# Another order of the steps in a two-layer graph kernel, with one buffer moved between two pools

## The chip, the core and the metric

The kernel runs on one core of one Trainium2 chip. The core has a matrix engine (TensorE, "PE" in the profile, with the loads of its stationary operand shown apart as "PEld"), three engines for elementwise work (VectorE "DVE", ScalarE "ACT", GpSimd "POOL") and a sync engine whose queue issues nearly all transfers ("SP"). PE writes its sums to eight banks of PSUM; DVE and ACT take them out to SBUF, where everything else lies. The metric is the device time of one execution in microseconds (us), taken as the median of several runs.

## The reference

The input is 128 graphs of 128 nodes with 512 features (`x`) and a 128 x 128 weighted adjacency matrix for each (`adj`). All numbers are 32-bit floats. Two layers follow each other, each with a residual sum and a layer norm:

```python
# layer 0
deg = sum(adj, -1);  agg = (adj @ x) / max(deg, 1e-6)
x = layernorm(x + relu(concat([x, agg]) @ W.T))            # W is 512 x 1024
# layer 1: three graph convolutions
h = relu(adj @ (x @ W1) + b1)
h = relu(adj @ (h @ W2) + b2)
x = layernorm(x + adj @ (h @ W3) + b3)                      # W1, W2, W3 are 512 x 512
```

So each graph meets five 512 x 512 weight matrices (the two halves of `W`, then `W1`, `W2`, `W3`) and its adjacency matrix four times.

## The kernel before

**Tiling.** Four graphs form a group, and there are NG = 32 groups. The large products are not done directly. They are done with the fast scheme that multiplies 2 x 2 blocks with seven products in place of eight, and for most of the weight matrices a second time inside each of the seven. The sums of blocks that the scheme needs are made ahead: by `sums` (outer level) and `inner_sums` (inner level, whose results go to small buffers called `ti`, three forms each). The inner forms of the two halves of `W` don't fit into SBUF and are streamed from device memory for every group, into a ring of six buffers (tiles `ring` and a part of `big`).

**Steps.** The work of one group is cut into 22 stages, whose names are used below:

- X, D, AT: load the transposed `x` and its sums; load the adjacency matrix and make the degrees; load the transposed adjacency matrix.
- L0 to L3: `x` times both halves of `W` (lines 875 to 878). L0 and L1 do the first four of the seven outer places, L2 and L3 the rest. A stage has seven products; a product of L is 4 matmul records of 256 columns (2 for L3).
- A0, A1: for two graphs each, adjacency times the result, relu, residual, layer norm (`seg_agg`, lines 880 to 903).
- G0 to G3: adjacency times the normalized result, one graph each (`seg_g1`).
- Ha, Hb: times `W1`, one level of the scheme only, so products of 8 records of 256 columns (line 596).
- Sa, Sb: times `W2`; H2: adjacency (`seg_h2`); Ta, Tb: times `W3`. A product is 8 records of 128 columns in Sa and Ta and 6 in Sb and Tb (line 614).
- Z0, Z1: adjacency, bias, residual, layer norm, and the way out (`seg_last`).

A stage is a generator, and each `yield` ends one step, mostly one product with what takes its result out of PSUM. In `first_part` (lines 630 to 665), which Sa, Ta, L0 and L1 use, the seven products come in the order 1, 5, 6, 2, 7, 4, 3. Products 1, 6, 7 and 4 add up in one bank, `py`, and ACT copies that bank out in between, so product 7 waits for the copy of what product 6 left (`copied`, line 576). `last_part` does the same for the other three places, and starts 5 from a bank that ACT fills first (line 698).

**Order.** Three things make the order of the instructions.

1. `ORDER` lists the steps of one period, 104 of them: `L3-4` means one step of stage L3 for the group that is four behind the period's number. A step whose stage is not yet allowed by `AFTER` goes to a list `late` and is taken as soon as it is allowed (lines 1218 to 1239). `AFTER` says what must be finished: Sa of a group needs Z0 and Z1 of the group before, Ha needs Tb of the group before, L0 needs A0 and A1 of the group before, and so on.
2. The list so made is a plan's input. `deadlines` (lines 78 to 93) gives each PE step a due time, the sum of the PE times ahead of it in the list, and every other operation the due time that its users leave it. An operation with no user is given `REST` us.
3. `order` (lines 95 to 223) plays the engines against each other with estimated durations. PE takes the first of its next `AHEAD` steps that is ready and has its buffers (lines 176 to 183). The other engines take the earliest due. DVE takes over a sum meant for POOL when it is due within `HELP` us (lines 191 to 196). A transfer or filling with a lead may not start more than that lead ahead of its due time: `LEADS` holds that for fillings of banks, loads of `x`, first inner sums and ring loads. The instructions are then put out in this order, and each engine runs its own in order.

**Buffers.** `SIZES` counts the `s` buffers (512 columns: banks copied out, loads of `x`, results on the way out), the `v` buffers (partial sums of a first part), the `ti` buffers (inner forms of the data) and the ring. A pair of places takes one `ti` buffer, so one operand of L, S or T takes four of them. The planner lets a load of `x` take an `s` buffer only when more than three are free.

Of the kernel before, what the change touches and what calls it, by code (L numbers as in the profile page):

```python
# [35 lines left out]
class Plan:  # L36
# [5 lines left out]


    LAG = 0.15
    AHEAD, HELP, HOLD, SEEN, REST, SPARE = 32, 16.0, 5.0, 8, 15.0, 1
    DMA_US, DMA_RATE = 2.0, 0.22e6

    def __init__(self, pools):
# [175 lines left out]


BANKS = 8
SIZES = 8, 3, 7, 6
LEADS = 6.9, 7.0, 29.0, 448.5
AFTER = {
    "X": "L2-1+1 L3-1+1", "D": "A0-1 A1-1 D-1", "AT": "Z0-2 Z1-2", "L0": "X D AT A1-1 A0-1 Z0-2 Z1-2", "L1": "L0", "L2": "L1", "L3": "L1 L2<2",  # L230
    "A0": "L2 L3", "A1": "L2 L3", "G0": "A0 Hb-1", "G1": "A0 Hb-1", "G2": "A1 Hb-1", "G3": "G0 G1 G2 A1",
    "Ha": "G3 Tb-1!", "Hb": "Ha", "Sa": "Hb Z0-1! Z1-1!", "Sb": "Sa", "H2": "Sb", "Ta": "H2", "Tb": "Ta", "Z0": "Ta Tb!", "Z1": "Tb",
}
ORDER = """
    L3-4 L0-4 Ta-6 H2-5 L3-4 Tb-5 Sa-5 L1-4 L1-4 Hb-5 D Tb-6 L2-4 L3-4 G0-4 Z0-6 Sb-4 D L2-4 L2-4 Tb-5 L0-3 L0-3 L1-4
    Ta-5 Ha-4 A1-4 L1-4 L3-3 Tb-5 Sb-4 X-3 Tb-5 A0-4 Ha-4 L2-4 L3-3 Ha-4 Ha-4 H2-5 H2-5 H2-5 Hb-4 L0-3 Tb-5 Tb-5 H2-5
    L3-4 L2-4 L2-4 Sb-4 L1-3 L2-4 L0-3 Z1-6 Sb-4 L3-3 Ta-5 Sb-4 Ta-5 G3-4 AT-3 A0-3 Ta-5 G2-4 Z0-5 L3-3 Z0-5 G2-4 Sa-4
    Ha-3 Ta-5 Tb-5 A1-4 Ha-3 Sb-4 G1-4 Sa-4 Sb-4 L0-3 G3-4 Sb-4 L1-3 Sa-4 Sa-4 Sa-4 Sa-4 Z1-5 A0-4 L1-3 G1-4 Z1-6 L2-3
    Hb-4 G0-4 AT-3 Ta-5 X-2 L1-3 Ta-5 L0-3 A1-3 Sa-4 L0-3
"""  # L240


# [1 line left out]
def gnn_resnorm_kernel(  # L244
# [24 lines left out]

    NS, NV, NI, NR = SIZES  # L270
    EARLY = 2
# [35 lines left out]
    def pinned(ins):  # L307
        return tc.keep_in_program_order(ins)
# [4 lines left out]
    def scalar(n, emit, reads, writes, columns=0, lead=None):  # L313
        plan.op("ACT", 0.165 + 0.00083 * n + 0.1 * columns, emit, reads, writes, lead=lead)

    def dma(dst, src, reads, writes, size, queue="SP", lead=None):
        eng = nc.sync if queue == "SP" else nc.scalar
        plan.op(queue, 0.06, lambda: pinned(eng.dma_start(dst(), src())), reads, writes, size=size, lead=lead)  # L318

    def const(v):  # L320
        return lambda: v

    def add(eng, n, dst, a, b, reads, writes, op=OP.add, shared=False, lead=None):

        on_vector = lambda: pinned(nc.vector.tensor_tensor(dst(), a(), b(), op=op))  # L325
        if eng == "POOL":
            on_gpsimd = lambda: pinned(nc.gpsimd.tensor_tensor(dst(), a(), b(), op=op))  # L327
            plan.op("POOL", 0.03 + 0.00243 * n, on_gpsimd, reads, writes, True, other=(0.06 + 0.00123 * n, on_vector), lead=lead)
        else:
            vector(n, on_vector, reads, writes, shared)  # L330
# [90 lines left out]
    class Streamed:  # L421

        def parts(self, ps, i):
# [3 lines left out]
                lambda: RING_T[s.index][:, 0:n], const(FORMS[i - 1][:, ps[0] : ps[-1] + 1].rearrange("p k s n -> p k (s n)")),  # L427
                ["ring free"] + [("form", w, i, p) for w in range(2) for p in ps], [s], n * P * H * 4, lead=LEADS[3],
            )
            return [lambda j=j: RING_T[s.index][:, j] for j in range(n)], [s]  # L430

    class Data:
# [18 lines left out]
        def inner_sums(self):  # L451
            for ps in PAIRS:
# [13 lines left out]
                for dst, a, b, reads, writes, op in (  # L466
# [4 lines left out]
                ):  # L471
                    add("POOL", n * P, dst, a, b, reads, writes, op, lead=LEADS[2] if dst is first else None)

# [91 lines left out]
    def bank_ap(s):  # L565
        return BANK[s.index]

    def quarters(p, n):
        return bank_ap(p).rearrange("p a (b n) -> p (a b) n", n=P)[:, 0:n]
# [50 lines left out]
    def v_part(v, n, g, c):  # L620
        return lambda: V_T[v.index][:, 0:n, g, c]
# [56 lines left out]
    def last_part(a, b, ps, joint, v, kv, sinks):  # L678
# [18 lines left out]

        scalar(n * P, lambda: pinned(nc.scalar.copy(quarters(pz, n), v_part(v, n, 1, 1)())), kv, [pz], lead=LEADS[0])
        add("POOL", n * P, v_part(v, n, 0, 1), v_part(v, n, 0, 1), v_part(v, n, 1, 1), kv, [(v, "d")], OP.subtract)
# [180 lines left out]
    def seg_agg(q, m):  # L880
        y, u = l0(q)
        for g in (2 * m, 2 * m + 1):
            p, r = Slot("bank", seeded=True), Slot("s", spare=3)
            dma(lambda r=r: S_T[r.index].rearrange("p a b -> p (a b)"), const(x[q][:, g]), (), [r], P * F * 4, lead=LEADS[1])
            scalar(512, lambda g=g, p=p: pinned(nc.scalar.copy(bank_ap(p), u.graph(g))), u.keys((g,)), [p], lead=LEADS[0])
            plan.op(
# [211 lines left out]
    def seg_last(q, m):  # L1098
# [3 lines left out]
        for j, o in enumerate(os):  # L1102
            g = 2 * m + j
            p = Slot("bank", seeded=True)
            scalar(512, lambda p=p: pinned(nc.scalar.copy(bank_ap(p).rearrange("p a b -> p (a b)"), B3_T)), ["b3"], [p], lead=LEADS[0])
            plan.op(
# [181 lines left out]
```

## Time and profile before

| | |
|---|---|
| median of 3 runs | 2265.83 us (2265.13 to 2266.15) |
| the profiled execution | 2261.35 us, its span 2259.4 us |
| PE busy | 2238.6 us (99%), 13620 matmul records |
| weight loads | 1967.4 us (87%) |
| DVE, ACT, POOL busy | 72%, 55%, 49% |
| DMA | 147 GB/s on average; the main queue's packets 47.5% of the 16 engines |

The span is what the profile's page covers; the execution's own time has 1.95 us more around it. The median of the runs is 4.5 us above the profiled execution. In the middle of the kernel the picture repeats every 69.59 us: the group of 44 records that begins at 1038 us of the chain is at 1107 and 1177 us again. This is the period, one group of graphs. A record's time as the page gives it includes the way through the array, so records overlap: a row of 8 records of 128 columns is listed with 1.06 us, and the next row begins 0.89 us after it began. Where the next row begins later than that, PE has lost time. This is how the rows below are to be read.

### The profile page before, as it was taken

Reading aid. Unit: us, or ns where it says so; the run is one execution under the profiler, and the core shown is the slowest. Engines: PE = TensorE matmul, PEld = TensorE weight load, DVE = VectorE, ACT = ScalarE, POOL = GpSimd, SP = SyncE. Lnnn points to the kernel's source line nnn. Section 1 sums busy time; section 2 is a strip of 40 time slices with the busy share of each in tenths; the row PEclk is TensorE's granted clock in tenths of the full one; section 3 lists DMA queues with packets and bytes.
Section 4 is the critical chain, followed back from the end, with each engine's and each line's share of the span. In section 5 each row is a group of like instructions: output and inputs, shape, how many; then the busy total and the mean of one; then the engine's idle time right before and its main releaser. Section 6 shows DMA issues by size and latency. Waiting matters only on the chain.

```text
span 2259.4 us, 39677 instructions
## 1 busy us (share of the span) xinstructions
PE 2238.6 (99%) x13620; PEld 1967.4 (87%) x13620; DVE 1632.7 (72%) x3552; ACT 1237.8 (55%) x2369; POOL 1112.0 (49%) x1400
## 2 busy tenths in 40 slices
PE   8999999999999999999999999999999999999998
PEld 7888888898898988988888889889898898888886
DVE  5677777777777777777777777777777777777675
ACT  2455555555555555555555555555555555555554
POOL 0245554545545455454555454654545545455540
PEclk9999999999999999999999999999999999999999
DMA  7744445534455444554444553445534455443431
GB/s 236 158 139 133 138 155 172 168 122 146 130 180 175 122 147 134 167 171 137 139 135 158 171 164 123 144 137 176 179 117 151 130 167 171 131 135 127 157 120 38
DMA packets 218615, 333.12 MB, mean 147 GB/s; under 512 B 39344, under 2 KB 84400, under 8 KB 218416
## 3 DMA queue, kind: packets, MB, share of 16 engines
q1 hardware_dynamic: 217744, 330.33, 47.5%
q8 instruction: 110, 1.80, 0.4%
q14 instruction: 89, 0.73, 0.2%
q10 hardware_dynamic: 672, 0.26, 0.1%
HBM read 290.46 MB, written 40.04 MB: 146 GB/s over the span
## 4 chain that ended last, share of the span: by engine, by line
PE 98%; DMA 1%; DVE 0%; issue 0%; ACT 0%; SPq 0%; ACTq 0%; DVEq 0%
PE bank L614 58%; PE bank L596 21%; PE bank L914 5%; PE bank L1002 5%; PE bank L1109 5%; PE bank L889 5%; DMA s<-in_x_dram 1%; DMA big<-in_w0T_dram 0%; DVE st L828 0%; DVE u L896 0%; DVE big L325 0%; SPq L318 0%; ACTq L1283 0%; ACT u L859 0%; ACT T L1013 0%
## 5 line engine op out<-in xcount | busy, mean ns | idle before, releaser
L576 ACT COPY s<-bank 128x384 f32<-128x384 f32 (+1 forms) x567 | 306.2, 540 | 428.7 <-PE bank L614 327.3
L596 PE MATMUL bank<-T,w 128*128 128x256 f32 x1792 | 411.7, 379 | 0.0
L596 PEld LDWEIGHTS bank<-T,w 128*128 128x128 f32 x1792 | 335.8, 190 | 68.9 <-issue 28.5
L327 POOL TENSOR_TENSOR xT<-xT 128x512 f32<-128x512 f32 (+1 forms) x244 | 236.6, 970 | 137.6 <-DVE ah L325 41.4
L325 DVE TENSOR_TENSOR v<-bank,s 128x512 f32<-128x512 f32 x240 | 162.7, 688 | 191.5 <-PE bank L614 133.9
L327 POOL TENSOR_TENSOR T<-T 128x512 f32<-128x512 f32 (+2 forms) x250 | 253.0, 1028 | 69.5 <-ACT T L925 38.1
L614 PE MATMUL bank<-big,ti 128*128 128x128 f32 (+1 forms) x1410 | 261.7, 317 | 0.0
L614 PE MATMUL bank<-big,xT 128*128 128x256 f32 x976 | 253.9, 380 | 1.1 <-DMA big<-forms 1.1
L582 ACT COPY bank<-bank 128x512 f32<-128x512 f32 (+2 forms) x273 | 142.9, 523 | 176.7 <-PE bank L614 124.4
L614 PEld LDWEIGHTS bank<-w,ti 128*128 128x128 f32 x1680 | 215.9, 192 | 18.9 <-issue 7.2
L614 PEld LDWEIGHTS bank<-big,T 128*128 128x128 f32 x1680 | 215.9, 191 | 15.5 <-issue 7.0
L327 POOL TENSOR_TENSOR v<-v 128x384 f32<-128x384 f32 (+2 forms) x90 | 88.9, 1002 | 284.0 <-DVE v L325 156.8
L614 PE MATMUL bank<-w,T 128*128 128x128 f32 x1680 | 228.2, 276 | 0.0
L614 PE MATMUL bank<-big,T 128*128 128x128 f32 x1680 | 223.9, 276 | 2.9
L614 PE MATMUL bank<-w,ti 128*128 128x128 f32 x1680 | 226.5, 275 | 0.0
L614 PEld LDWEIGHTS bank<-w,T 128*128 128x128 f32 x1680 | 213.6, 192 | 10.4 <-ACT bank L582 5.7
L614 PEld LDWEIGHTS bank<-big,ti 128*128 128x128 f32 x1410 | 204.6, 191 | 18.6 <-issue 4.8
L325 DVE TENSOR_TENSOR row<-bank,s 128x384 f32<-128x384 f32 (+2 forms) x254 | 118.8, 468 | 136.8 <-PE bank L614 91.8
L325 DVE TENSOR_TENSOR T<-T 128x512 f32<-128x512 f32 (+1 forms) x370 | 208.8, 585 | 4.9 <-ACT T L925 4.2
L327 POOL TENSOR_TENSOR s<-s,v 128x512 f32<-128x512 f32 (+1 forms) x60 | 68.1, 1135 | 282.1 <-DVE T L325 165.3
L614 PEld LDWEIGHTS bank<-big,xT 128*128 128x128 f32 x976 | 174.7, 190 | 19.6 <-DMA big<-forms 1.7
L325 DVE TENSOR_TENSOR v<-v 128x512 f32<-128x512 f32 (+1 forms) x270 | 179.1, 672 | 8.5 <-DVE v L325 0.5
(86 smaller groups left out, 4095.2 us busy)
## 6 DMA issues: line engine op xcount, KB each, us to landing
big<-forms SPq DMA_DIRECT2D x327, 256.0 KB, 3.7
ring<-forms SPq DMA_DIRECT2D x303, 256.0 KB, 3.7
s<-in_x_dram SPq DMA_DIRECT2D x128, 256.0 KB, 5.1
out_dram<-s SPq DMA_DIRECT2D x126, 256.0 KB, 3.5
xT<-in_xT_dram SPq DMA_DIRECT2D x62, 512.0 KB, 5.8
big<-forms SPq DMA_DIRECT2D x119, 128.0 KB, 2.2
ring<-forms SPq DMA_DIRECT2D x91, 128.0 KB, 2.7
ar<-in_adj_dram SPq DMA_DIRECT2D x32, 256.0 KB, 2.8
```

Of the source, the lines that this page charges most:

```text
L325: on_vector = lambda: pinned(nc.vector.tensor_tensor(dst(), a(), b(), op=op))
L327: on_gpsimd = lambda: pinned(nc.gpsimd.tensor_tensor(dst(), a(), b(), op=op))
L576: scalar(n * P, lambda: pinned(nc.scalar.copy(quarters_of(s, n), quarters(p, n))), [p], [s])
L582: scalar(n * P, lambda: pinned(nc.scalar.copy(quarters(s, n), quarters(p, n))), [p], [s])
L596: nc.tensor.matmul(bank_ap(p)[:, o, :], lhsT, rhs, start=start and o == 0 and c == 0, stop=c == 1, skip_group_check=True,)
L614: nc.tensor.matmul(dst, ta(), tb(), start=start and n == 0, stop=True, skip_group_check=True)
L889: nc.tensor.matmul(bank_ap(p), AH_T[:, g, :], y.graph(g), start=False, stop=True, skip_group_check=True)
L914: nc.tensor.matmul(bank_ap(p)[:, c // 2, (c % 2) * P : (c % 2 + 1) * P], u.chunk(g, c), a[:, g, :], start=c == 0, stop=True, skip_group_ch ...
L1002: nc.tensor.matmul(bank_ap(p)[:, g // 2, (g % 2) * P : (g % 2 + 1) * P], s.chunk(g, o), a[:, g, :], start=g == 0, stop=True, skip_group_ch ...
L1109: nc.tensor.matmul(bank_ap(p), a[:, g, :], s.graph(g), start=False, stop=True, skip_group_check=True)
```

## The change

The change touches three sets of constants and nothing else. No operation is added or taken away.

- The planner's constants: PE looks over 20 steps in place of 32, DVE helps within 12 us in place of 16, and operations without users are due after 40 us in place of 15.
- The buffers: nine `s` in place of eight, six `ti` in place of seven. The leads: fillings of banks 8.2 us (6.9), first inner sums 30.7 us (29.0), ring loads 456 us (448.5).
- The order: 104 steps as before, each stage as often as before, at other places and with other lags.

```diff
-    AHEAD, HELP, HOLD, SEEN, REST, SPARE = 32, 16.0, 5.0, 8, 15.0, 1
+    AHEAD, HELP, HOLD, SEEN, REST, SPARE = 20, 12.0, 5.0, 8, 40.0, 1
...
-SIZES = 8, 3, 7, 6
-LEADS = 6.9, 7.0, 29.0, 448.5
+SIZES = 9, 3, 6, 6
+LEADS = 8.2, 7.0, 30.7, 456.0
...
 ORDER = """
-    L3-4 L0-4 Ta-6 H2-5 L3-4 Tb-5 Sa-5 L1-4 L1-4 Hb-5 D Tb-6 L2-4 L3-4 G0-4 Z0-6 Sb-4 D L2-4 L2-4 Tb-5 L0-3 L0-3 L1-4
-    Ta-5 Ha-4 A1-4 L1-4 L3-3 Tb-5 Sb-4 X-3 Tb-5 A0-4 Ha-4 L2-4 L3-3 Ha-4 Ha-4 H2-5 H2-5 H2-5 Hb-4 L0-3 Tb-5 Tb-5 H2-5
-    L3-4 L2-4 L2-4 Sb-4 L1-3 L2-4 L0-3 Z1-6 Sb-4 L3-3 Ta-5 Sb-4 Ta-5 G3-4 AT-3 A0-3 Ta-5 G2-4 Z0-5 L3-3 Z0-5 G2-4 Sa-4
-    Ha-3 Ta-5 Tb-5 A1-4 Ha-3 Sb-4 G1-4 Sa-4 Sb-4 L0-3 G3-4 Sb-4 L1-3 Sa-4 Sa-4 Sa-4 Sa-4 Z1-5 A0-4 L1-3 G1-4 Z1-6 L2-3
-    Hb-4 G0-4 AT-3 Ta-5 X-2 L1-3 Ta-5 L0-3 A1-3 Sa-4 L0-3
+    L1-4 L3-3 D Sa-4 G2-3 L2-4 L0-3 Ta-6 L2-4 Hb-5 L2-4 Ha-4 L0-3 Tb-6 Ta-5 L1-4 L3-2 L1-4 Tb-5 L3-4 Ha-4 L1-4 G3-4
+    L2-3 L1-3 Z0-5 D Sa-3 Sb-3 Z1-6 Tb-5 Z1-5 G3-4 Sa-4 H2-5 L0-2 Tb-5 Sb-3 L3-4 H2-5 Sa-3 H2-5 H2-5 AT-3 L2-4 L1-3
+    Hb-4 Tb-5 Tb-5 L3-3 L3-4 G2-4 G1-4 L0-3 G0-3 L0-2 Z0-3 Sb-4 Ha-4 L2-4 L3-3 X-2 A1-4 Ta-5 A0-4 Ta-5 A0-4 Sa-4 Hb-2
+    Ta-5 A1-4 A0-4 Ha-3 L0-2 G1-3 AT-3 Sb-2 Ta-5 Z1-6 H2-4 X-1 Sb-3 Ta-5 Tb-5 Ha-3 L3-3 Sa-4 G0-2 L2-3 Sb-2 L1-3 Sb-4
+    Sa-4 Sb-2 Ha-3 Sa-3 L0-2 Ta-5 A1-3 L2-3 Z0-5 Tb-4 L1-2 L0-2
 """
```

## The prediction

> **What bounds the kernel.** I read the page's head, then busy time by stretch, then who waited for whom, then PE's timeline of one period. The page:
>
> ```profile
> span 2259.4 us, 39677 instructions
> ...
> PE 2238.6 (99%) x13620; PEld 1967.4 (87%) x13620; DVE 1632.7 (72%) x3552; ACT 1237.8 (55%) x2369; POOL 1112.0 (49%) x1400
> ```
>
> Busy time in stretches of 69 us (PE first): the start, the middle, the last.
>
> ```profile
> 0.00:69.00 69.00, 62.73 (x280) 53.11 (x281) 39.04 (x82) 22.42 (x37) 6.97 (x9) 1.00 0.83 228
> ...
> 1035.00:1104.00 69.00, 68.90 (x430) 60.97 (x429) 51.32 (x113) 38.89 (x75) 37.07 (x49) 1.00 0.49 152
> ...
> 2208.00:2277.00 69.00, 42.89 (x209) 34.85 (x207) 25.89 (x57) 22.86 (x44) 0.91 (x1) 0.96 0.09 31
> ```
>
> In the middle PE is busy 68.90 of 69 us, at full clock. It is the bound; only what PE loses counts. The waits of its weight loads say where:
>
> ```profile
> PEld bank L889 <- ACT bank L885: 8.0, 32, 0.3
> PEld bank L614 <- POOL T L327: 7.4, 31, 0.2
> PEld bank L614 <- ACT bank L582: 5.7, 30, 0.2
> ```
>
> About 31 times each: once a period. Whether PE loses anything by them is seen in its timeline. This is the stretch where no L product is left for PE, so it is the thinnest of the period:
>
> ```profile
> 1000.65 1.05 PE L614 MATMUL bank<-w,T 128*128 128x128 f32 x8
> 1001.54 1.08 PE L614 MATMUL bank<-big,xT 128*128 128x256 f32 x4
> 1002.46 1.11 PE L614 MATMUL bank<-w,T 128*128 128x128 f32 x8
> 1003.41 1.03 PE L614 MATMUL bank<-ring,ti 128*128 128x256 f32 x4
> 1004.27 3.60 PE L889 MATMUL bank<-row,ah 128*128 128x512 f32 x8
> 1007.71 1.05 PE L614 MATMUL bank<-w,ti 128*128 128x128 f32 x8
> 1008.60 1.06 PE L614 MATMUL bank<-big,ti 128*128 128x128 f32 x8
> 1009.49 0.83 PE L614 MATMUL bank<-w,T 128*128 128x128 f32 x6
> 1010.42 1.13 PE L614 MATMUL bank<-big,T 128*128 128x128 f32 x8
> 1011.39 0.83 PE L614 MATMUL bank<-big,ti 128*128 128x128 f32 x6
> ```
>
> By the pace of undisturbed rows, 8 records of 128 columns take 0.89 us from start to start, 6 take 0.67 and 4 of 256 take 0.86. Here the starts are 0.92 (0.06 lost), 0.95 (0.06), 0.93 after a row of six (0.26), and 0.97 (0.08): 0.46 us a period. The largest loss, explained by ACT and PEld:
>
> ```profile
> 1007.28 0.19 PEld L614 LDWEIGHTS bank<-w,ti 128*128 128x128 f32 x1 [0.24 <-POOL T L327]
> 1009.69 0.58 ACT L576 COPY s<-bank 128x512 f32<-128x512 f32 x1 [3.65 <-PE bank L614]
> 1010.39 0.97 PEld L614 LDWEIGHTS bank<-big,T 128*128 128x128 f32 x8 [0.26 <-issue]
> ```
>
> Rows 1008.60 and 1010.42 are Ta's products 6 and 7, with only Tb's first (six records, 0.67) between. Product 7 needs the bank's copy: 0.20 from 1009.49 to ACT's start, 0.58 for the copy, 0.12 to the load, 0.90 in all against 0.67 of cover. That product 7 waits for the copy is my reading of the code; the profile calls it "issue".
>
> **The budget.** In the same way PE's timeline gives: 5.4 us before the first matmul; half pace (427 ns for 256 columns against 216) and one wait of 0.85 up to 13.7 us; waits of 1.1 (first streamed forms) and 2.0 us (layer norm of group 1) at 106 and 110 us; 30 periods x 0.46 = 13.8 us; 0.7 us at 2249; and 7.8 us from the last matmul to the end. The change can touch 1.1 + 2.0 + 13.8 + 0.7 = 17.6 us, 0.8% of the time. That is the limit of a gain; there is none for a loss.
>
> **What the Trainium skill says.** "Perfetto Trace Analysis", Identifying the Most-Contended Engine, warns that matmul busy time overstates how near PE is to its limit, and prefers the share of weight loads. Here that is 87%, but the starts leave only 0.46 us in 69.59, so I trust the starts. The same page, Optimization Strategy, says that a bubble that repeats can mean too few buffers; here the repeated bubble stands behind a copy, which a buffer does not shorten. "SBUF — State Buffer", SBUF: two separate sides, says that DVE and GpSimd share a port pair as an exclusive lock. The trace agrees: in the view of the ti tiles, the same DVE sum of 256 columns is 417 ns at the median on T and 1317 ns on xT, where it stands beside POOL's. So a sum moved between them is not free for the other.
>
> **The change, part by part.** Instructions, records and transfers stay the same in number: 0 us.
>
> *Order.* Carrying out `ORDER` with `AFTER`, as lists without any times, most tokens find their stage not yet allowed and run in bursts, so the two lists differ less than they look. Both run: Tb, then Z0 and Ha, Hb, then Sa among L0 and L1, Sb, L2 with L3, H2, the A steps, Ta, the G steps. What moves: (a) Z0's first product goes ahead of Ha; (b) Sa's last product goes behind L1's first three; (c) both xT loads and their sums go ahead of the A steps, not among them: on SP the second then passes one or two ring issues of 0.32 us each. Now it is issued at 1004.57, lands some 5.8 us later, and the sums on xT begin at 1013.4: 3 us of margin hide it, and the ring issues behind it run far ahead of their use; (d) the A steps A0 A1 A1 A0, with four Ta steps behind them, become A1 A1 Ta A0 Ta A0 Ta. Only (d) lies in the thin stretch. An A product is 0.86 us (3.44 for four). One of them between Ta's products 6 and 7 covers the missing 0.23 wholly: 0.26 + 0.08 saved, x 30 = -10.2 us. PE may use the A products up earlier, since it takes whatever is ready: then 0. I take -10.2, and +3 for one new loss of 0.1 a period, of the size of the two small ones that exist.
>
> *AHEAD 20.* A period has 79 PE steps, so 32 covers 28 us and 20 covers 17.6. Cost 0 while one of 20 is ready; the cover is L's products, absent from 1004.3 to 1018.8. Without it a step waits at the rate of a copy, 0.2 to 0.9 us.
>
> *HELP 12.* Sums return from DVE to POOL. Per sum of 256 columns that is 0.73 for 0.42. In the forecast 0, hidden by Tb's product (0.67) that PE can take meanwhile; without that cover, rival 2.
>
> *REST 40.* Results go out up to 25 us later in due time; each SP issue then stands behind loads (0.32 us each), and no one waits for it but the `s` buffer. The ninth buffer pays for that: 0. Layer norm of Z on DVE and ACT gives way to others: slightly below 0, not counted.
>
> *Six `ti`.* xT holds four from 1304 to 1326 us while h1's sums take a fifth and sixth at 1318 and a seventh at 1321.5. With six, that third pair waits for L0's release at about 1326, some 4 us. Its first user, Sb, comes at 1331.9, after about 2 us of sums: 4 us of margin left for the fourth pair. h2's four at 1349 to 1358 stand beside two of L: six fit. Taken as 0; range 0 to 1 us a period, 30 us.
>
> *Leads.* Filled banks are held 1.3 us longer, of eight banks; 0, up to the 0.1 us of a small loss.
>
> Sum against the profiled span: 2259.4 - 10.2 + 3 = 2252.2, or -7.2 us. Against the median: 2265.8 - 7.2 = 2258.6, since the median is only 4.5 us above the profiled execution and I assume that this stays.
>
> **Rivals.**
> 1. *The bubble only moves* (0.22). PE uses the A products up while POOL finishes h2's sums (it waits for POOL at 1007.28 now), and product 7 comes as late as before, or Tb's does. For: the planner takes any ready step. Against: the A steps are due later now. Then -4 to +4.5 us: 2262 to 2270.
> 2. *POOL's sums of h2 become late* (0.33), slower. Ta's product 5 starts at 1007.71, right behind POOL's last sum of T; its load already waited 0.24 with PE still covered. DVE made two of these sums (1003.33, 1007.01). With less help, each costs about 0.3 more, and the chain is 0.6 us late; a blocked port adds the same again. PE's cover there is Tb's 0.67. So it decides once the slip passes about 0.3 us beyond what (d) saves: 0.15 to 1 us a period, +4.5 to +30 us, in the middle +12: 2278. The six `ti` would show the same way at Sb.
> 3. *The change does nothing to PE's idle time*, because every moved step is hidden behind PE's other work, as nearly all waits of the other engines are now: this is the centre of rival 1, 2266, and shares its chance.
>
> **Numbers.** A difference under 0.2% (4.5 us) is about what a measurement here can't tell from none. Forecast 0.45: 2249 to 2261, likeliest 2258.6. The chance of faster is 0.45 and little from rival 1: 0.46. Same: most of rival 1, 0.20. Slower: 0.34. The range leaves out gains beyond 17 us (2249) and the upper fifth of rival 2: 2249 to 2284. The forecast's own range is 2249 to 2261.
>
> **What the profile after would show.** Right: the period is below 69.5 us, and in the timeline an A row stands between Ta's products 6 and 7, with no "issue" gap behind the copy. Rival 1: a period within 0.15 us of 69.59 with the gap elsewhere. Rival 2: more PEld time waiting for POOL than 7.4 us in all, longer than 0.24 each, and a period above 69.74; POOL's share above 49%. What would make it wrong otherwise: a transfer of the ring or of xT that lands late, seen as a PE wait for DMA in the middle, where now there is none; or new losses in the first 130 us, where the first streamed forms arrive.

## The result, and the profile after

The changed kernel takes 2258.59 us (median of 9 runs, 2257.20 to 2260.22). The kernel before took 2265.83 us in 9 runs beside it (2261.82 to 2267.45). The ratio is 0.9969, with a 95% interval of 0.9960 to 0.9977: 0.31% faster. The profiled execution took 2258.39 us, only 3.0 less than the one before (2261.35), where the medians differ by 7.2. This matters below.

The head of the page, and the busy time of the second 69 us and of the middle (PE, PEld, DVE, ACT, POOL, clock, DMA share, GB/s):

```profile
span 2256.6 us, 39998 instructions
...
PE 2235.8 (99%) x13620; PEld 1966.1 (87%) x13620; DVE 1612.9 (71%) x3559; ACT 1238.6 (55%) x2369; POOL 1069.8 (47%) x1393
```

```profile
69.00:138.00 69.00, 63.59 (x304) 53.76 (x303) 41.19 (x93) 28.68 (x56) 24.09 (x27) 0.95 0.39 93
...
1035.00:1104.00 69.00, 69.00 (x430) 60.89 (x429) 50.21 (x113) 39.09 (x75) 35.02 (x46) 1.00 0.48 151
```

The second 69 us of before:

```profile
69.00:138.00 69.00, 65.89 (x325) 55.34 (x324) 44.66 (x100) 30.75 (x60) 20.67 (x23) 1.00 0.50 116
```

The middle is full (69.00 of 69 us, 68.90 before). The second 69 us are worse: PE was busy 65.89 us there before and is busy 63.59 now, at a mean clock of 0.95. So the change won in the period and lost in the first 130 us, which I call the ramp.

The waits of the weight loads, as engine, line and releaser: us in total, times, the longest.

```profile
PEld bank L1109 <- DVE row L325: 19.9, 29, 0.7
...
PEld bank L914 <- ACT u L859: 5.8, 1, 5.8
...
PEld bank L889 <- ACT bank L885: 0.7, 2, 0.4
PEld bank L614 <- POOL T L327: 0.5, 2, 0.2
```

The loads that stood behind POOL's sums of T (7.4 us, 31 times before) and behind L885 (8.0, 32 times) hardly wait. A new wait stands at Z, line 1109, once a period.

PE's timeline of the thin stretch:

```profile
1004.66 1.05 PE L614 MATMUL bank<-w,T 128*128 128x128 f32 x8
1005.55 1.02 PE L889 MATMUL bank<-row,ah 128*128 128x512 f32 x2
1006.41 1.05 PE L614 MATMUL bank<-w,ti 128*128 128x128 f32 x8
1007.30 1.88 PE L889 MATMUL bank<-row,ah 128*128 128x512 f32 x4
1009.02 1.05 PE L614 MATMUL bank<-big,ti 128*128 128x128 f32 x8
1009.91 1.02 PE L889 MATMUL bank<-row,ah 128*128 128x512 f32 x2
1010.78 0.83 PE L614 MATMUL bank<-w,T 128*128 128x128 f32 x6
1011.44 1.06 PE L614 MATMUL bank<-big,T 128*128 128x128 f32 x8
1012.34 0.83 PE L614 MATMUL bank<-big,ti 128*128 128x128 f32 x6
```

Ta's product 6 starts at 1009.02 and product 7 at 1011.44. An A product (1009.91) now stands between them beside Tb's first, and the row after Tb's begins 0.66 us after it, at the undisturbed pace. Product 7's load waits for nothing, and the copy of the bank was done 0.62 us before it:

```profile
1010.12 0.59 ACT L576 COPY s<-bank 128x512 f32<-128x512 f32 x1 [2.91 <-PE bank L614]
...
1011.33 0.97 PEld L614 LDWEIGHTS bank<-big,T 128*128 128x128 f32 x8
```

The ramp, from the timeline of all engines (SPq is SP issuing transfers):

```profile
91.08 0.17 DVE L554 RECIPROCAL deg<-deg 128x4 f32<-128x4 f32 x1
...
91.28 0.38 SPq L318 DMA_DIRECT2D dd<-deg  x1
...
91.75 1.41 SPq L318 DMA_DIRECT2D s<-in_x_dram  x3
...
105.86 0.69 DVE L896 SCALAR_TENSOR_TENSOR u<-bank,s 128x512 f32<-128x512 f32 x1 [8.96 <-DMA s<-in_x_dram]
...
109.76 3.75 PE L914 MATMUL bank<-at,u 128*128 128x128 f32 x16 [5.41 <-ACT u L859]
```

Group 3's degrees go out to device memory (`dd<-deg`), and three loads of `x` for group 1 stand behind that issue on SP. The first of them lands 14 us later, DVE and ACT wait for it, and PE is idle for 5.4 us. The 16 records after it take 3.75 us; an undisturbed row of 16 takes 1.95, so this costs another 1.8. The Trainium skill, "TensorE: Matmul & The Clock Gate", What's actually happening, says that the clock falls to half after an idle window of about 3.4 us and comes back after as much busy time. The trace agrees on the fall and on the return: PE's pace is half from 109.76 to 113.3 us, 3.6 us. It does not agree on the length of the idle time: PE's last row ended at 104.35, the granted clock is 1.00 up to 106.5 us and 0.51 from there to 113.4, so it fell after some 2.2 us. Experiment 1 has more such cases.

The kernel before has the same late loads: its loads of `x` stand behind the degrees too (issued at 90.79), and the two whose landing the trace has took 11.0 and 13.0 us. But PE there runs products with streamed forms at 106.7 to 108.7 us, ahead of this row, and its idle time is in two pieces, 1.1 and 2.0 us, with the clock at 1.00 throughout:

```profile
110.69 2.94 PE L914 MATMUL bank<-at,u 128*128 128x128 f32 x24 [2.00 <-ACT u L859]
```

So the delay was there already, and the change took away PE's cover for a part of it.

**Where PE loses time.** For the whole trace I take each record's distance to the next start, less the undisturbed 111, 216 or 429 ns for 128, 256 or 512 columns, and add up by stretch (us; 130 to 2225 are 30 periods). The last three rows are experiments below.

| | 0–80 | 80–130 | 130–2225 | later |
|---|---|---|---|---|
| before | 4.8 | 3.7 | 18.0 | 0.9 |
| after | 4.9 | 7.4 | 11.0 | 1.0 |
| after, A products bunched | 4.7 | 9.8 | 20.8 | 0.9 |
| before, group 3's degrees on ACT's queue | 5.2 | 0.0 | 21.1 | 0.9 |
| after, group 3's degrees on ACT's queue | 4.0 | 0.0 | 11.8 | 0.9 |

Between 130 and 2225 us the change saves 7.0, between 80 and 130 it loses 3.7, and the first matmul starts 0.4 later: -2.9, which is what the two profiled executions differ by. A period is 69.34 us (69.59). Added up in the same way, every kernel here with the new list and group 3's degrees on SP loses 7.4 to 10.8 us between 80 and 130 us, and every such one with the old list 2.3 to 5.9. So the loss in the ramp came with the list.

### The profile page after: what moved, and what is told of

Read it like the earlier page. It is cut to its first block, busy times and chain, and to the rows that moved or that the text cites. A ratio compares the mean times of both kernels' runs of the same rounds, so it can differ in the third digit from the quotient of the medians.

```text
span 2256.6 us, 39998 instructions
## 1 busy us (share of the span) xinstructions
PE 2235.8 (99%) x13620; PEld 1966.1 (87%) x13620; DVE 1612.9 (71%) x3559; ACT 1238.6 (55%) x2369; POOL 1069.8 (47%) x1393
## 4 chain that ended last, share of the span: by engine, by line
PE 98%; DMA 1%; DVE 0%; SPq 0%; ACT 0%; issue 0%; ACTq 0%; DVEq 0%
PE bank L614 57%; PE bank L596 21%; PE bank L914 5%; PE bank L1109 5%; PE bank L1002 5%; PE bank L889 5%; DMA s<-in_x_dram 1%; DMA ar<-in_adj_dram 0%; SPq L318 0%; DMA big<-forms 0%; DVE st L828 0%; DVE u L896 0%; ACT u L859 0%; DVE s L325 0%; DVE T L325 0%
## 5 line engine op out<-in xcount | busy, mean ns | idle before, releaser
L327 POOL TENSOR_TENSOR xT<-xT 128x512 f32<-128x512 f32 (+1 forms) x244 | 247.4, 1020 | 76.9 <-DVE rstd L840 35.9
L614 PE MATMUL bank<-big,ti 128*128 128x128 f32 (+1 forms) x1430 | 268.2, 319 | 0.0
L582 ACT COPY bank<-bank 128x512 f32<-128x512 f32 (+2 forms) x273 | 143.1, 524 | 209.0 <-PE bank L614 162.9
L614 PEld LDWEIGHTS bank<-big,ti 128*128 128x128 f32 x1430 | 212.3, 191 | 32.2 <-issue 20.2
L325 DVE TENSOR_TENSOR T<-T 128x512 f32<-128x512 f32 (+2 forms) x407 | 233.1, 597 | 7.3 <-ACT T L925 6.3
L614 PEld LDWEIGHTS bank<-w,ti 128*128 128x128 f32 x1680 | 218.3, 192 | 20.5 <-issue 13.6
L327 POOL TENSOR_TENSOR T<-T 128x512 f32<-128x512 f32 (+2 forms) x213 | 193.8, 930 | 70.5 <-DVE T L325 46.1
L614 PE MATMUL bank<-big,xT 128*128 128x256 f32 x870 | 224.2, 380 | 0.2 <-DMA big<-forms 0.2
L614 PE MATMUL bank<-ring,xT 128*128 128x256 f32 x810 | 211.9, 380 | 0.0
L325 DVE TENSOR_TENSOR v<-v 128x512 f32<-128x512 f32 (+1 forms) x299 | 190.0, 643 | 1.0
L327 POOL TENSOR_TENSOR v<-v 128x384 f32<-128x384 f32 (+1 forms) x61 | 69.3, 1136 | 248.4 <-DVE u L325 129.3
L327 POOL TENSOR_TENSOR ti<-T 128x256 f32<-128x256 f32 (+1 forms) x150 | 90.5, 622 | 189.7 <-DVE T L325 112.4
```

Of the source, the lines that this page charges most:

```text
L582: scalar(n * P, lambda: pinned(nc.scalar.copy(quarters(s, n), quarters(p, n))), [p], [s])
L614: nc.tensor.matmul(dst, ta(), tb(), start=start and n == 0, stop=True, skip_group_check=True)
```

## The experiments

**1. One part alone, order only.** The kernel before with the new `ORDER`, nothing else.

```diff
 ORDER = """
-    L3-4 L0-4 Ta-6 H2-5 L3-4 Tb-5 Sa-5 L1-4 L1-4 Hb-5 D Tb-6 L2-4 L3-4 G0-4 Z0-6 Sb-4 D L2-4 L2-4 Tb-5 L0-3 L0-3 L1-4
...
+    L1-4 L3-3 D Sa-4 G2-3 L2-4 L0-3 Ta-6 L2-4 Hb-5 L2-4 Ha-4 L0-3 Tb-6 Ta-5 L1-4 L3-2 L1-4 Tb-5 L3-4 Ha-4 L1-4 G3-4
...
```

> The kernel before with the new list of steps alone. In its order of instructions an A product stands between Ta's products 6 and 7 (cover 0.86 + 0.67 us against the 0.90 that the copy needs). Theory (the copy's missing cover is what the change removes, and the list does it): no gap there, the period at or below 69.35 us, 2258 us (2255 to 2261). Rival (planner's constants or the buffers bring the gain): period 69.59, 2266 us. If the list also brings losses that the new constants removed: between the two, with new gaps in PE's timeline.

Measured: 2400.59 us, ratio 1.0605 (1.0584 to 1.0625). The forecast missed by 140 us. The gap behind product 6 did close; another wait came. Two lines of the waits (engine, line, releaser: us, times, longest) and one period of the timeline:

```profile
PE bank L614 <- DVE row L325: 80.6, 25, 4.6
...
DVE deg L552 <- DMA dd<-deg: 125.4, 26, 6.2
```

```profile
491.64 0.39 SPq L318 DMA_DIRECT2D dd<-deg  x1
...
500.42 0.69 DVE L552 TENSOR_REDUCE deg<-ar 128x4 f32<-128x512 f32 x1 [4.18 <-DMA dd<-deg]
...
501.62 0.94 PE L614 MATMUL bank<-w,ti 128*128 128x128 f32 x6 [2.52 <-DVE row L325]
```

In D, the next group's reduction comes close behind this group's degrees on their way out. DVE waits for their landing (issued 491.64, 8.8 us), Tb's row sums stand behind DVE, and PE behind those. The waits cost more than their 80.6 us: the granted clock is 0.50 from 502.6 to 506.0 us, behind the one shown, and so it is for 3.4 us (once 6.8) behind 21 of the 25. That adds some 38 us. The 21 are idle times of PE from 2.5 to 4.6 us; the four others were 2.1 to 2.8 us. So there is no sharp limit here, and 2.5 us can be enough.

**2. That cause, tested.** The same, with the planner told that this transfer takes 6.2 us more, so that DVE does something else meanwhile. Nothing else differs.

```diff
-        dma(const(dd.rearrange("g i -> i g")), const(d), kd, [("dd", q % 2)], 400000 if q else 1600000, queue)
+        dma(const(dd.rearrange("g i -> i g")), const(d), kd, [("dd", q % 2)], 400000 if q else 1600000, queue, late=6.2 if q > 1 else 0.0)
```

> The new list alone, as in the run that took 2400.6 us, with one more edit: the planner is told that the small transfer of the degrees to device memory takes 6.2 us more than it assumes, so that it lands in about 10 us as the traces show. Theory (the list alone is slow because the reduction of degrees stands in DVE's queue behind that transfer, 125 us of waits, and Tb's row sums stand behind it): the waits of DVE for that transfer fall below 10 us, PE's 80 us of waits for row sums go, and the time falls to 2256 to 2270 us. Rival (the long wait is only where DVE was going to be idle, and the list without the ninth s buffer and the shorter window is slow by itself): still above 2350 us.

Measured: 2284.40 us, 1.0086 (1.0072 to 1.0099), above the forecast. DVE's wait fell from 125.4 to 21.2 us, and PE's for the row sums vanished: 116 of the 135 us were this one wait and the half clock behind it. It is not all. Small gaps remain in each period, such as this one, and a ramp wait of 7.7 us:

```profile
PE bank L614 <- ACT bank L698: 4.8, 29, 0.2
```

**3. The planner's constants alone, and the buffers alone.**

```diff
-    AHEAD, HELP, HOLD, SEEN, REST, SPARE = 32, 16.0, 5.0, 8, 15.0, 1
+    AHEAD, HELP, HOLD, SEEN, REST, SPARE = 20, 12.0, 5.0, 8, 40.0, 1
```

> The kernel before with the new AHEAD, HELP and REST alone. In its order of instructions the four A products stand in a row as before, but Ta's product 2 is no longer used up early: between products 6 and 7 stand product 2 (0.89) and Tb's first (0.67). Theory of cover: the gap of 0.26 + 0.08 closes here too, period about 69.3, 2257 to 2260 us. Rival (only the A product placed there closes it): 2266. Rival 2 of the prediction (less help on DVE makes POOL late): above 2268, PE waiting for POOL.

```diff
-SIZES = 8, 3, 7, 6
-LEADS = 6.9, 7.0, 29.0, 448.5
+SIZES = 9, 3, 6, 6
+LEADS = 8.2, 7.0, 30.7, 456.0
```

> The kernel before with the new buffer counts and leads alone. Between Ta's products 6 and 7 stand product 2 and Tb's first, as with the constants alone. Theory of cover: 2257 to 2260 us, the gap closed. Rival (six ti buffers cost up to 1 us a period at Sb): above 2268.

Measured: 2322.67 us, 1.0254 (1.0239 to 1.0269), and 2331.84 us, 1.0294 (1.0279 to 1.0309). Both forecasts missed. PE's waits with the constants alone:

```profile
PE bank L614 <- DVE T L325: 13.2, 15, 0.9
PE bank L614 <- ACT bank L698: 9.3, 15, 0.6
PE bank L614 <- DMA ring<-forms: 8.8, 14, 1.1
```

And with the buffers alone:

```profile
PE bank L614 <- DVE T L325: 26.4, 30, 0.9
```

In both, Ta's first product waits for the sums of h2, by up to 0.9 us. This is the place of the prediction's rival 2, with DVE, not POOL, as the late one. In both PE also waits for ring loads in the middle (7.0 us in all with the buffers alone), which the prediction had named as a sign of being wrong. PE's waits come to 31 and 33 us, about half of what the middle loses more than before; the rest is in smaller gaps and in slow first records behind the waits.

**4. One part taken back.** The kernel after with the old constants, and with the old buffers and leads.

```diff
-    AHEAD, HELP, HOLD, SEEN, REST, SPARE = 20, 12.0, 5.0, 8, 40.0, 1
+    AHEAD, HELP, HOLD, SEEN, REST, SPARE = 32, 16.0, 5.0, 8, 15.0, 1
```

> The changed kernel with the planner's three constants as before: new list and new buffers. Its order of instructions in the thin stretch is that of the changed kernel. Theory (the list closes the gap behind product 6, and the rest only has to keep the reduction of degrees off the transfer): near the changed kernel, 2255 to 2265 us, if the wait for that transfer does not come back; with it back, 2300 to 2400 us. Rival (the shorter window and the smaller help are needed for the gain): above 2266 us with waits of other kinds.

```diff
-SIZES = 9, 3, 6, 6
-LEADS = 8.2, 7.0, 30.7, 456.0
+SIZES = 8, 3, 7, 6
+LEADS = 6.9, 7.0, 29.0, 448.5
```

> The changed kernel with buffers and leads as before: new list and new planner's constants. Theory as for the other half: 2255 to 2270 us if the wait of DVE for the transfer of the degrees stays under 10 us in all, 2300 to 2400 if it is back as with the list alone. Rival (the ninth s buffer is what the gain needs): above 2270 us, with waits for loads of x.

Measured: 2285.82 us, 1.0091 (1.0076 to 1.0106), and 2313.29 us, 1.0218 (1.0202 to 1.0234). With the old constants DVE's wait for the degrees does not come back (1.3 us), so the theory's 2255 to 2265 us failed and its rival came: one gap in every period.

```profile
PE bank L614 <- ACT bank L582: 19.8, 30, 0.7
```

With the old buffers that wait is back, and the time lies where the expectation put that case:

```profile
PE bank L614 <- ACT s L576: 18.3, 30, 0.6
PE bank L596 <- DVE row L325: 17.5, 12, 2.7
...
DVE deg L552 <- DMA dd<-deg: 42.2, 25, 3.6
```

So none of the three parts is neutral. Alone they cost 135, 57 and 66 us; together they save 7. Taking back the constants costs 27 us, the buffers 55. Which of the three constants closes the gap at L582, and which buffer or lead the others, was not tried.

**5. Part (d) taken back.** The kernel after with the A steps together and the Ta steps behind them.

```diff
-    Hb-4 Tb-5 Tb-5 L3-3 L3-4 G2-4 G1-4 L0-3 G0-3 L0-2 Z0-3 Sb-4 Ha-4 L2-4 L3-3 X-2 A1-4 Ta-5 A0-4 Ta-5 A0-4 Sa-4 Hb-2
+    Hb-4 Tb-5 Tb-5 L3-3 L3-4 G2-4 G1-4 L0-3 G0-3 L0-2 Z0-3 Sb-4 Ha-4 L2-4 L3-3 X-2 A1-4 A0-4 A0-4 Ta-5 Ta-5 Sa-4 Hb-2
```

> The changed kernel with one thing undone in its list: the A steps stand in a row again, A1 A1 A0 A0 Ta Ta Ta. In its order of instructions only Tb's first product (0.67) stands between Ta's products 6 and 7. Theory: the gap of 0.26 + 0.08 us is back in every period, 30 x 0.34 = +10 us, 2266 to 2270 us. Rival (the gain has nothing to do with that place): 2258.6, no change.

Measured: 2268.18 us, 1.0010 (1.0004 to 1.0017); 9.6 us more than the kernel after. The gap is back in every period, with its size of before (rows of PE and ACT):

```profile
1017.32 1.06 PE L614 MATMUL bank<-big,ti 128*128 128x128 f32 x8
1018.22 0.83 PE L614 MATMUL bank<-w,T 128*128 128x128 f32 x6
1018.42 0.59 ACT L576 COPY s<-bank 128x512 f32<-128x512 f32 x1 [3.80 <-PE bank L614]
1019.15 1.13 PE L614 MATMUL bank<-big,T 128*128 128x128 f32 x8
```

From 1018.22 to 1019.15 are 0.93 us where six records take 0.67: 0.26 lost, and 0.07 after it. Times 30 that is 10 us. That the stretch from 130 to 2225 us loses just 9.8 more is in part chance, since the planner wrote a new order around the moved steps (POOL has 1480 instructions, 1393 in the kernel after): two small gaps of the kernel after (5.8 us) are gone and others of about that size came.

**6. Is it the copy that product 7 waits for?** The profile called that wait "issue". Here the kernel before makes this one copy, in Sa and Ta, in four quarters, with PE's order unchanged. The added code shifts lines 576 and 614 to 584 and 624.

```diff
-        s2 = copied(py)
+        s2 = copied(py) if joint else copied_in_quarters(py)
...
+            return [pinned(nc_.copy(quarters_of(s, 4)[:, i], quarters(p, 4)[:, i])) for i in range(4)][-1]
```

> The kernel before, with the same order of PE's instructions, and ACT's copy behind product 6 of Sa and Ta made in four quarters in place of one piece, which takes longer. Theory (product 7 of Ta waits for that copy): one copy of 128 columns takes about 0.27 us, so the copy takes about 1.0 us in place of 0.58, and the gap behind Tb's first product grows from 0.26 to some 0.7 us; 30 periods give +13 us, 2275 to 2283 us. Rival (product 7 waits for something else, the profile calls it issue): the gap stays at 0.26 us and the time within 3 us of 2266.

```profile
1014.44 0.83 PE L624 MATMUL bank<-w,T 128*128 128x128 f32 x6
1014.64 0.77 ACT L584 COPY s<-bank 128x128 f32<-128x128 f32 x4 [3.65 <-PE bank L624]
...
1015.55 1.13 PE L624 MATMUL bank<-big,T 128*128 128x128 f32 x8 [0.28 <-ACT s L584]
```

Measured: 2271.56 us, 1.0025 (1.0017 to 1.0033), +6.1 us where I expected 13. The mechanism holds: four quarters take 0.77 us where one copy took 0.58, and the gap grew by the same 0.19, from 0.26 to 0.45, times 30 = 5.6 us. I had put the four quarters at 1.0 us together. The profile now names the copy.

**7. The ramp: are the streamed forms in the way?** The kernel after with its first six loads of inner forms held back to a lead of 28 us.

```diff
-                s], n * P * H * 4, lead=LEADS[3],
+                s], n * P * H * 4, lead=LEADS[3] if self.count > 6 else 28.0,
```

> The changed kernel with the first six loads of streamed forms held back to 28 us ahead of their use, so that they don't share the transfer engines with the loads of x of group 1 at 92 to 106 us. Theory (PE's idle 5.6 us at 104 us, and the half clock behind it that costs 1.9 us, come from the landing of these loads of x in 14 us): both shrink, 2250 to 2255 us. Rival (the layer norm's chain or the queue ahead of the loads sets that time): no change, 2258.6 us, or a wait for the streamed forms at 136 us in its place.

Measured: 2261.41 us, 0.9983 (0.9976 to 0.9989). A miss: `x` still takes 13.7 us to land, and PE waits 5.0. But the run says nothing on the forms, for the six loads did not move. They begin at 93.21 us in the kernel after, and here (the first three):

```profile
93.23 8.10 SPq L318 DMA_DIRECT2D big<-forms  x3
```

What speaks against the forms is experiment 8, where they are issued right behind the loads of `x`, from 88.3 us, and `x` is not late. The edit did make the planner order the early instructions anew, with 2.8 us of new gaps in the middle: the whole of the difference to the kernel after.

**8. The ramp: is it the transfer of degrees?** Group 3's degrees are issued from ACT's queue, in the kernel after and in the kernel before. PE's order is untouched in both.

```diff
-        dma(const(dd.rearrange("g i -> i g")), const(d), kd, [("dd", q % 2)], 400000 if q else 1600000, queue)
+        dma(const(dd.rearrange("g i -> i g")), const(d), kd, [("dd", q % 2)], 400000 if q else 1600000, "ACT" if q in (0, 3) else "SP")
```

> The changed kernel with one transfer moved: the small transfer of the degrees of group 3, which SP issues at 91.3 us just ahead of three loads of x, goes out on ACT's queue. Theory (those loads land in 14 us because they stand behind that transfer in SP's queue, and PE's idle 5.6 us at 104 us, with 1.9 us at half clock behind it, follows from that): the loads land in about 5 us, both losses shrink to under 2 us, 2250 to 2254 us. Rival (the loads are slow because the first streamed forms share the engines, or the waits of SP itself set the time): no change, 2258.6 us.

> The kernel before with the one transfer of degrees of group 3 issued from ScalarE's queue; PE's order is that of the kernel before. In the profiled execution of the kernel before, the ramp cost 1.1 us (first streamed forms) and 2.0 us (layer norm of group 1), and its runs spread over some 2262 to 2271 us with a median 4.5 us above the profiled one. If that spread is the ramp's (how late the loads of x behind the degrees land, and whether the clock then falls), the median falls below 2261 us and the runs lie within 4 us of each other: 2256 to 2261. If the ramp cost only what the profiled execution shows, the median falls by 2 to 3 us to 2262 to 2264 and the spread stays. If the degrees' place on SP does not matter in the kernel before, 2265 to 2267. In all three the gap of 0.26 us behind Ta's product 6 stays, with a period of 69.59 us.

Measured: the kernel after falls to 2251.57 us, 0.9933 (0.9921 to 0.9946): 7.0 below the kernel after, and the best of all. The kernel before falls to 2261.87 us, 0.9984 (0.9976 to 0.9992). In the kernel after with this edit SP no longer stands at the degrees, and the loads of `x` go first:

```profile
86.44 1.81 SPq L318 DMA_DIRECT2D s<-in_x_dram  x4
90.07 0.37 ACTq L318 DMA_DIRECT2D dd<-deg  x1
...
106.49 1.95 PE L914 MATMUL bank<-at,u 128*128 128x128 f32 x16
```

They land after 4.9 us at the median, and the stretch from 80 to 130 us loses nothing, in the kernel before as well (table above). The kernel before falls by 3.7 us against the runs beside it (2265.58), which is its loss there in the table; the expectation had 2262 to 2264 for that case. But its profiled execution took 2261.18 us, where that of the kernel before took 2261.35, although 3.7 us of ramp are gone. The difference is in two of its periods, at 1090 and 1787 us, where a copy by ACT came late:

```profile
PE bank L596 <- ACT bank L582: 2.0, 2, 1.1
```

Experiment 6, which also has PE's order of before, loses 0.65 to 1.2 us in this way five times; the profiled execution of the kernel before has none, nor have those of after and of after with this edit. What makes that copy late I could not find in the trace. It would explain that the runs of before lie 4.5 us above its profiled one and spread, and the fall by just 3.7 us says that this distance is not in the ramp. But the other runs have no profile: that stays open.

**9. Another queue, or another place in time?** All transfers of degrees on ACT's queue, in the kernel after.

```diff
-        dma(const(dd.rearrange("g i -> i g")), const(d), kd, [("dd", q % 2)], 400000 if q else 1600000, queue)
+        dma(const(dd.rearrange("g i -> i g")), const(d), kd, [("dd", q % 2)], 400000 if q else 1600000, "ACT")
```

> The kernel after with the transfer of degrees of every group issued from ScalarE's queue. With group 3 alone moved it took 2251.6 us. If the degrees matter only in the ramp, the same: 2250 to 2254 us with a period of 69.33 us. If ScalarE, which runs its instructions in order, now waits for VectorE's degrees in every period with copies of banks queued behind it, PE shows new waits for ScalarE's copies and it is slower by 0.1 to 0.8 us a period: 2255 to 2275 us.

Measured: 2280.67 us, 1.0065 (1.0052 to 1.0077), 22 us more than the kernel after and beyond the slower case. Its cause is another too. Early on, the degrees now go out just ahead of group 0's loads of `x`, on the other queue:

```profile
41.77 0.43 ACTq L318 DMA_DIRECT2D dd<-deg  x1
...
42.93 0.97 SPq L318 DMA_DIRECT2D s<-in_x_dram  x2
...
55.99 1.29 DVE L896 SCALAR_TENSOR_TENSOR u<-bank,s 128x512 f32<-128x512 f32 x2 [16.20 <-DMA s<-in_x_dram]
56.74 0.80 PE L596 MATMUL bank<-big,xT 128*128 128x256 f32 x1 [7.00 <-DVE u L896]
```

Those two loads land after 13.0 us although they are on SP's queue. So it is not the queue that counts, but whether the degrees are ahead when the loads are issued. Up to 80 us the run loses 8.4 us more than the kernel after. PE's one long wait for ACT is 5.6 us in the ramp, behind a layer norm, and not in the middle. The middle loses 13.6 us more than in the kernel after; there DVE waits for the degrees again (58.4 us, 26 times), and PE for DVE's row sums (9.6 us, 7 times).

## Why the prediction was right, and where it was not

The predicted time, 2258.6 us, was met, and the mechanism that it rests on is shown. That it was met so closely is luck: two other terms were wrong and cancelled.

- **Order (d), -10.2 us: right in place and size.** The A row stands between products 6 and 7; the gap of 0.26 + 0.07 is gone in 30 periods (10 us); undoing (d) costs 9.6, with other small gaps about in balance. Experiment 6 shows that the "issue" gap was the copy.
- **One new small loss, +3 us: right only as a balance.** Two came. One is at Z (line 1109, behind DVE's row sum): PE loses 0.13 in 29 periods, 3.7 us. The other is 0.07 in a row of eight records (at 1054.65), 2.1 us. And the two small losses of before, 3.2 us in all, are gone, which the working did not have. In sum the middle gained 7.0 us; the working said 7.2. Part (a), which moves Z, does not bring the loss at Z alone: experiments 2 and 5 have the same Z steps and not that wait.
- **Order (c), 0: right.** PE waits for no xT load.
- **AHEAD, HELP, REST, Six *ti*, Leads, each 0: wrong as separate terms.** Only their sum with the new order is near 0. My reasons looked for a cover in the old schedule (the margin of 4 us for a third pair, the cover of L's products). But each constant makes the planner write out a whole new order, and what decides is which waits meet in it. HELP shows it: with the constants alone 53 sums moved from DVE to POOL, as the prediction said (1400 to 1453 instructions of POOL), and in the whole change seven moved the other way (1393).
- **The budget's ramp, "there is none for a loss": the loss came there.** Between 80 and 130 us the loss went from 3.7 to 7.4 us. The prediction named new losses in the first 130 us as what could make it wrong, but with the streamed forms as their source; experiment 8 shows the loads of `x` behind the degrees.
- **"The median is only 4.5 us above the profiled execution and I assume that this stays": wrong.** It is 0.2 us after. The profiled executions differ by 3.0, not 7.2. The ramp's loss is in every run of after, for the fastest of them (2257.20) is above the slowest with group 3's degrees moved (2252.57), and the runs of before carried some 4 us that its profiled execution did not have. With the ramp's loss taken from both (experiment 8), the medians differ by 10.3 us. I had the right sum from one error of about +4 and one of about -4.
- **Rival 1** did not happen; experiment 5 is what it would have looked like (most periods at 69.59 us and a median of 2268). **Rival 2** did not happen in the change: PEld's wait for POOL fell from 7.4 to 0.5 us and POOL's share to 47%. Its weight was not idle: late sums of h2 came in both kernels of experiment 3.

## What to carry to other kernels

When a planner writes the order, its constants, buffer counts and step list are one setting: judge them together, and don't add up the effects of single edits. A gap behind a copy out of PSUM is closed by one more independent product between the two that share the bank, and the starts of PE's rows show it even where the profile says only "issue". Before adding a saving to a median, look at whether the profiled execution stands for the runs, and look at the ramp on its own.

## What the runs showed of the hardware that I had not expected

The transfer of degrees is 2 KB, but it lands late, and it holds back what is issued after it. In the kernel after, a window of the DMA view around one in the middle (181.5 to 193 us, nearly nothing else moving) and its row among the issues (KB each, median us to landing, from the window 84 to 108 us):

```profile
DMA packets 534, 0.02 MB, mean 2 GB/s; under 512 B 530, under 2 KB 530, under 8 KB 533
```

```profile
dd<-deg SPq DMA_DIRECT2D x1, 2.0 KB, 12.2
```

It is cut into some 530 tiny packets. It lands after 9.4 us at the median of the 12 whose landing the trace has, and after 12.2 us in the ramp, where a 256 KB load of `x` takes 4.9 at the median. Of the three loads behind it, the one that DVE waits for took 14.0 us: it landed at 105.8, 2.3 us after the degrees (91.28 + 12.2 = 103.5). The Trainium skill, "DMA: Bandwidth & Descriptors", says in Specifications that pieces under 512 B are written by read-modify-write, and in Queues, rings and completion order that a transfer's completion signal is written only after all earlier writes of the same DMA engine, across its queues. Experiment 9 agrees with "across its queues"; that read-modify-write is what makes the degrees late, no run here shows. But a late signal is not all, for the data of the loads is late too. The same view from 93 to 103 us, while the degrees are on their way, and from 103 to 108 us:

```profile
DMA packets 61, 0.12 MB, mean 12 GB/s; under 512 B 0, under 2 KB 0, under 8 KB 61
```

```profile
DMA packets 864, 1.58 MB, mean 315 GB/s; under 512 B 95, under 2 KB 95, under 8 KB 864
```

In those 10 us only 61 packets of 2 KB start, where a load of `x` has 128, and the engines count as busy for 41% of the time. What holds the packets up is not in the trace.
